# A paged-attention layer: new keys transposed by VectorE with the first queries, new values moved to matching partitions

## The chip, the cores and the metric

The kernel runs on one core of a Trainium2 chip. The metric is the device time of one launch in microseconds (us): the median of several runs. The engines of a core are TensorE (PE in the profile, with its weight loads as PEld), VectorE (DVE), ScalarE (ACT), GpSimd (POOL) and SyncE (SP, which here only issues DMAs). Sixteen DMA engines move data.

## The reference

Eight sequences of 128 tokens with 512 channels go through two residual layers, all in float32. The first adds a per-sequence adapter product (LoRA). The second is grouped-query attention over a paged cache: 32 query heads share 8 key and value heads, and every query sees up to 512 cached keys, those below the sequence's length, and its 128 new keys.

```python
w = weight[adapter_ids]                          # 512 x 512 for each sequence
x = x + einsum('bsi,boi->bso', x, w)
q, k, v = x @ Wq.T, x @ Wk.T, x @ Wv.T           # 32, 8, 8 heads of 128
q, k = rope(rmsnorm(q) * q_norm_w), rope(rmsnorm(k) * k_norm_w)
k_all = concatenate([k_cache[block_table], k])   # 512 cached + 128 new keys
v_all = concatenate([v_cache[block_table], v])
scores = q @ k_all.T * SCALE                     # masked beyond the length
o = softmax(scores) @ v_all                      # each kv head serves 4 query heads
x = x + o @ Wo.T
```

## The kernel before

The work is cut into 32 steps, 4 groups of heads times 8 sequences. A step (g, b) handles 8 query heads and 2 key/value heads (j = 0, 1) of one sequence. The main loop (L981) runs over the steps, and within a step over 8 slots, one for each query head h, where j = h // 4 and r = h % 4. Four heads with the same j form a unit.

In a slot TensorE first makes the head's scores (L1031): a matmul over the 512 cached keys and one over the 128 new keys. In the trace each of the float32 matmuls is two passes. VectorE adds the mask and finds the smallest score (L1041; the queries are negated). ScalarE takes the exponential (L1057), VectorE the reciprocal of the sum (L1098), and GpSimd scales (L1105). One slot later VectorE transposes the 128 x 640 result p in blocks of 32 x 32 (`turn_p`, L871). Such blocks don't make a full transpose: the blocks must still change partitions. So when the four heads of a unit are through, `send` (L889) writes them to DRAM, and in the next slot `receive` (L898) reads them back rearranged as pT, with keys on partitions. A value matmul needs pT (`values`, L825; named o<-pT).

The rest of TensorE's work fills the slots as a list of pieces, `main`: the projections of the next step (pj_kv, pj_q), the values of the step before (o), and its output product (out). A planner gives each piece a cost (`UNIT` = 0.86) and spreads the pieces evenly over the slots that are left. Small transposes are put at fixed slots by `at(step, slot, early, function, n)` with a cost of n x 0.11, which the planner counts.

There are two ways to transpose an operand. Cached keys and queries mostly go the way of p: VectorE turns 32 x 32 blocks, SyncE's DMA queue writes them to DRAM and reads them back (`send_k` L782, `receive_k` L796, `send_q` L804). The new keys instead go through TensorE: `turn_k` (L759) transposes one 128 x 128 head with the identity, and ScalarE copies it from PSUM into kT's last part (L764). It is called twice for each step, at slot 6 of the step before for j = 0 and at slot 2 for j = 1 (L266, L268). For the first, second and last step the queries too are turned by TensorE (`by_pe`, L637).

The block transposes leave the keys of a sequence in a particular order: after turning, key position i of block a comes from row 4i + a. In kT that order is a, c, i (block, chunk of 128 keys, position), and the mask, key_no and p have the same order. So the new keys have to be written in the matching order too. That is done in `rotate` (L639), where GpSimd adds the two halves of the rotary embedding with strided output (L671), the `turned_order` branch. The new values, vn, are copied by ScalarE as they are (L716).

Projections' follow-up work is put on a list, `pending`, and run at the next slot. DMA receives go on the list `to_read` with the slot they were asked in, and are issued a slot later, in order of a second number:

```python
due = [r for r in to_read if r[0] < 8 * i + h]
for _, _, f in sorted(due, key=lambda r: r[1]):
    f()
```

SyncE issues in program order and holds everything behind a DMA that still waits. Its order within a late step: in slot 0 the send of the second unit of the step before (xp) and kT for j = 1; in slot 1 that unit's pT and the send of the next step's cached keys (xk); in slot 3 the send of the next step's first queries (xq); in slot 4 the send of the first unit, the first queries' receive (qT) and the next kT for j = 0; in slot 5 the first unit's pT; in slot 6 the send of the second queries, and in slot 7 their receive. ScalarE issues the weight DMAs and GpSimd the gathers of cached keys and values.

Of the kernel before, what the change touches and what calls it, by code (L numbers as in the profile page):

```python
# [18 lines left out]
P = 128  # L19
# [33 lines left out]
def lora_then_paged_attention(  # L53
# [155 lines left out]
    for a in range(4):  # L209
# [9 lines left out]

    key_no = const.tile([P, 4, LC, Q4], FP, name="key_no")  # L220
    nc.gpsimd.iota(
        key_no,
        pattern=[[1, 4], [P, LC], [4, Q4]],
        base=0,
# [4 lines left out]
    nc.gpsimd.memset(mhalf, -0.5)  # L229
    masks = [const.tile([P, 4, NC, Q4], FP, name=f"mask_{n}") for n in range(2)]  # L230
    for m in masks:
        nc.gpsimd.memset(m[:, :, LC, :], 0.0)

# [154 lines left out]
    def rope_angles():  # L388
# [7 lines left out]
        def temp(tag):  # L396
            t = work.tile([P, 4, D], FP, tag=tag, name=f"rope_{tag}")
            return t.rearrange("p h (u d) -> p (h u) d", u=2)

# [200 lines left out]
    class Step:  # L600
        def __init__(self):
            self.kT, self.qT, self.q, self.pT, self.oT = {}, {}, {}, {}, {}
            self.scaled = set()

# [24 lines left out]
    def make_mask(i):  # L629

        b = steps[i][1]
        nc.vector.tensor_scalar(
            masks[i % 2][:, :, 0:LC, :], key_no, len_f[:, b : b + 1], FAR, ALU.is_ge, ALU.mult
        )
# [4 lines left out]
    def rotate(i, y, dst, ss, table, n, between=None):  # L639
# [11 lines left out]

        turned_order = i > 0 and (table == 1 or (i, n) in by_pe)
        cw = dst
        if turned_order and table:
            cw = sw[:, 2 : 2 + heads, :]
        elif turned_order:
            cw = work.tile([P, 4, D], FP, tag=f"tq{n}", name=f"cw_{i}_{n}")
        nc.vector.tensor_tensor(
# [22 lines left out]
    def norm_scales(i, n, width):  # L681
# [22 lines left out]
    def project(i, what):  # L704
# [3 lines left out]
        def after_kv(y):  # L708
            s.k = work.tile([P, GK, D], FP, tag="k", name=f"k_{i}")
            s.vn = news.tile([P, GW], FP, tag="vn", name=f"vn_{i}")  # L710
            s.ss = [
                small.tile([P, 6], FP, tag=f"ss{n}", name=f"ss_{i}_{n}") for n in range(2)
            ]

            def rest():
                nc.scalar.copy(s.vn, y[:, GW : 2 * GW])  # L716
                rotate(i, y, s.k, s.ss[0][:, 4:6], 1, 0)

            pending.append(rest)

        def after_q(n):
            def after(y):
                s.q[n] = work.tile([P, 4, D], FP, tag=f"q{n}", name=f"q_{i}_{n}")

                def rest():
                    rotate(
                        i,
                        y,
                        s.q[n],
                        s.ss[n][:, 0:4],  # L730
# [16 lines left out]
    def turn_kc(i, j, copy=None):  # L747

        s = st[i]
        s.kT[j] = work.tile([P, 4, NC, Q4], FP, tag=f"kT{j}", name=f"kT_{i}_{j}")  # L750
# [6 lines left out]
        (copy or nc.scalar.copy)(s.kT[j][:, :, 0:LC, :].rearrange("d a c i -> d c a i"), t)  # L757

    def turn_k(i, j, copy=None):  # L759
        s = st[i]  # L760
        t = ps_mm.tile([P, HID], FP, tag="mm", name=f"kt_{i}_{j}")
        t = t[:, 0:P].rearrange("d (i a) -> d i a", a=4)
        nc.tensor.transpose(t.rearrange("d i a -> d (i a)"), s.k[:, j, :], ident)  # L763
        (copy or nc.scalar.copy)(s.kT[j][:, :, LC, :].rearrange("d a i -> d i a"), t)  # L764

# [30 lines left out]
    def receive_k(i, j):  # L796
        s = st[i]
        s.kT[j] = work.tile([P, 4, NC, Q4], FP, tag=f"kT{j}", name=f"kT_{i}_{j}")
        nc.sync.dma_start(
            out=s.kT[j][:, :, 0:LC, :].rearrange("d b c k -> d b (c k)"),  # L800
            in_=s.xk[:, :, j, :].rearrange("b d x -> d b x"),
        )
# [171 lines left out]
    turn_q(0, 0, on_act)  # L974
    turn_k(0, 0, on_act)
    for _ in range(3):
# [4 lines left out]
    for i, (g, b) in enumerate(steps):  # L981
# [38 lines left out]
        for h in range(8):  # L1020
# [8 lines left out]
            sc = ps_sc.tile([P, 1024], FP, tag="sc", name=f"sc_{i}_{h}")  # L1029
            for lo, hi in ((0, L), (L, LA)):  # L1030
                nc.tensor.matmul(  # L1031
                    sc[:, lo:hi],
                    lhsT=s.qT[j][:, r, :, :].rearrange("d h q -> d (h q)"),
                    rhs=s.kT[j].rearrange("d a c i -> d (a c i)")[:, lo:hi],
                    start=True,
# [7 lines left out]
                in0=sc[:, 0:LA],  # L1043
                in1=masks[i % 2].rearrange("p a c i -> p (a c i)"),
                scale=1.0,
# [54 lines left out]
            if i == last and j == 1:  # L1100

                unit.p[r] = probs.tile([P, LA], FP, tag="p", name=f"pk_{h}")
                p = p.rearrange("q (a c i) -> q a c i", a=4, c=NC)
                q = unit.p[r].rearrange("q (c i a) -> q a c i", a=4, c=NC)
            nc.gpsimd.tensor_scalar(q, p, unit.rc[:, one], 1.0, ALU.mult, ALU.mult)  # L1105
# [77 lines left out]
```

## Time and profile before

| | |
|---|---|
| runs | 1197.11, 1199.97, 1198.83 us; median 1198.83 |
| profiled execution | 1197.03 us, span 1194.7 us |
| TensorE clock granted | 1.00 |
| VectorE busy | 733.6 us (61%) |
| ScalarE busy | 531.5 us (44%) |
| GpSimd busy | 674.9 us (56%) |
| DMA | 328.02 MB, mean 275 GB/s |
| queue 1 (SyncE's) | 239.23 MB, 59.6% of 16 engines' span |
| queue 10 (ScalarE's) | 48.12 MB, 12.4% |
| queue 0 (GpSimd's) | 39.86 MB, 10.1% |

A group in the profile reads: line, engine, operation, output<-inputs, shapes, count | busy us, mean ns of one | idle time of the engine before them, and what ended it. Busy time is the union of the durations, so overlapping instructions count once. A timeline row has start, duration, engine, line, operation, tensors and count. The row of a stretch has its bounds and length, then each engine's busy time and count (PE, PEld, DVE, ACT, POOL), the granted clock, the DMA engines' mean share and GB/s; this share sums the packets' durations, so packets that overlap on an engine can take it above 1.

### The profile page before, as it was taken

Reading aid. Unit: us, or ns where it says so; the run is one execution under the profiler, and the core shown is the slowest. Engines: PE = TensorE matmul, PEld = TensorE weight load, DVE = VectorE, ACT = ScalarE, POOL = GpSimd, SP = SyncE. Lnnn points to the kernel's source line nnn. Section 1 sums busy time; section 2 is a strip of 40 time slices with the busy share of each in tenths; the row PEclk is TensorE's granted clock in tenths of the full one; section 3 lists DMA queues with packets and bytes.
Section 4 is the critical chain, followed back from the end, with each engine's and each line's share of the span. In section 5 each row is a group of like instructions: output and inputs, shape, how many; then the busy total and the mean of one; then the engine's idle time right before and its main releaser. Section 6 shows DMA issues by size and latency. Waiting matters only on the chain.

```text
span 1194.7 us, 12971 instructions
## 1 busy us (share of the span) xinstructions
PE 1178.0 (99%) x3412; PEld 576.4 (48%) x3412; DVE 733.6 (61%) x1675; ACT 531.5 (44%) x1648; POOL 674.9 (56%) x781
## 2 busy tenths in 40 slices
PE   7899999999999999999999999999999999999998
PEld 4554455454444444444444444444444444444454
DVE  5566656665566666766566676666657655565651
ACT  4564444444444444444444444444444444444432
POOL 5566455545566556555655556565556556655540
PEclk9999999999999999999999999999999999999999
DMA  8388788877988988888998998888898987777761
GB/s 290 110 278 273 261 292 293 275 261 246 309 289 301 334 303 300 294 270 300 296 303 280 340 313 298 298 278 300 267 319 277 303 285 264 243 255 242 260 222 60
DMA packets 187148, 328.02 MB, mean 275 GB/s; under 512 B 13124, under 2 KB 106052, under 8 KB 178116
## 3 DMA queue, kind: packets, MB, share of 16 engines
q1 hardware_dynamic: 124272, 239.23, 59.6%
q10 hardware_dynamic: 49524, 48.12, 12.4%
q0 software_dynamic: 13280, 39.86, 10.1%
q8 instruction: 27, 0.44, 0.2%
q14 instruction: 45, 0.37, 0.1%
HBM read 195.04 MB, written 132.12 MB: 274 GB/s over the span
## 4 chain that ended last, share of the span: by engine, by line
PE 97%; DMA 1%; ACT 1%; DVE 0%; POOL 0%; issue 0%; ACTq 0%; DVEq 0%; POOLq 0%
PE o L559 23%; PE sc L1031 23%; PE pj_q L559 18%; PE out L559 18%; PE pj_kv L559 9%; PE y L559 2%; PE lw L474 1%; DMA w_q<-xw_q 1%; PE x L474 1%; PE kt L763 1%; PE wt_q L492 0%; PE wt_kv L492 0%; PE qt L772 0%; PE wt_o L492 0%; PE pt L881 0%
## 5 line engine op out<-in xcount | busy, mean ns | idle before, releaser
L1041 DVE CUSTOM_DVE_ANT_0 p<-sc,mask 128x640 f32<-128x640 f32 x256 | 210.9, 824 | 400.5 <-PE sc L1031 400.4
L1057 ACT ACTIVATE p<-p,mn 128x640 f32<-128x640 f32 x256 | 211.6, 827 | 324.6 <-DVE mn L1041 322.4
L1031 PE MATMUL sc<-kT,qT 128*128 128x512 f32 (+1 forms) x1024 | 318.4, 433 | 1.1 <-ACT kT L764 0.8
L1105 POOL TENSOR_SCALAR p<-p,rc 128x640 f32<-128x640 f32 x252 | 201.9, 801 | 183.0 <-DVE rc L1098 181.0
L1031 PEld LDWEIGHTS sc<-kT,qT 128*128 128x128 f32 x1024 | 189.9, 190 | 226.4 <-issue 206.0
L559 PE MATMUL pj_q<-w_q,x1T 128*128 128x512 f32 x512 | 236.9, 593 | 1.4 <-ACT w_q L493 0.7
L559 PE MATMUL o<-pT,vc 128*128 128x512 f32 x512 | 236.9, 593 | 0.0
L559 PE MATMUL out<-w_o,oT 128*128 128x512 f32 (+1 forms) x528 | 234.9, 580 | 0.9 <-ACT oT L838 0.7
L871 DVE STREAM_TRANSPOSE tp<-p 128x640 f32<-128x640 f32 x252 | 211.0, 837 | 4.9 <-POOL p L1105 4.7
L610 POOL DMA_INDIRECT kc<-in_L_cond_k_cache_dram,key_ix x128 | 130.8, 1022 | 32.7 <-issue 32.5
L610 POOL DMA_INDIRECT vc<-in_L_cond_v_cache_dram,val_ix x128 | 127.9, 999 | 31.0 <-issue 30.8
L692 ACT ACTIVATE q<-q,rs 128x128 f32<-128x128 f32 x256 | 81.9, 390 | 139.1 <-POOL q L679 134.5
L559 PEld LDWEIGHTS out<-w_o,oT 128*128 128x128 f32 x528 | 95.7, 190 | 93.5 <-issue 89.9
L559 PEld LDWEIGHTS pj_q<-w_q,x1T 128*128 128x128 f32 x512 | 92.4, 190 | 93.8 <-issue 91.4
L559 PEld LDWEIGHTS o<-pT,vc 128*128 128x128 f32 x512 | 91.9, 190 | 88.6 <-issue 81.3
L559 PE MATMUL pj_kv<-w_kv,x1T 128*128 128x512 f32 x256 | 116.6, 593 | 0.7 <-ACT x1T L476 0.7
L671 POOL TENSOR_TENSOR k<-sw 128x256 f32<-128x256 f32 x31 | 22.9, 739 | 157.1 <-PE kt L763 133.4
L679 POOL TENSOR_TENSOR q<-q,sw 128x512 f32<-128x512 f32 x59 | 74.7, 1266 | 45.0 <-DVE sw L662 44.9
L646 ACT ACTIVATE sq<-pj_q 128x128 f32<-128x128 f32 x256 | 70.8, 277 | 50.4 <-PE pj_q L559 41.5
L687 POOL TENSOR_TENSOR rs<-ss,mhalf 128x6 f32<-128x6 f32 x64 | 77.6, 1212 | 5.3
L559 PEld LDWEIGHTS pj_kv<-w_kv,x1T 128*128 128x128 f32 x256 | 45.9, 190 | 45.6 <-issue 44.7
L559 PE MATMUL o<-pT,vn 128*128 128x512 f32 x128 | 65.4, 593 | 0.0
(123 smaller groups left out, 873.6 us busy)
## 6 DMA issues: line engine op xcount, KB each, us to landing
xp<-tp SPq DMA_DIRECT2D x63, 1280.0 KB, 5.9
pT<-xp SPq DMA_DIRECT2D x63, 1280.0 KB, 7.0
xk<-tk SPq DMA_DIRECT2D x31, 512.0 KB, 7.5
kT<-xk SPq DMA_DIRECT2D x62, 256.0 KB, 6.6
xq<-tq SPq DMA_DIRECT2D x59, 256.0 KB, 4.6
qT<-xq SPq DMA_DIRECT2D x59, 256.0 KB, 5.2
st_q<-in_L_cond_Wq_dram ACTq DMA_DIRECT2D x24, 256.0 KB, 5.3
xw_q<-tw_q ACTq DMA_DIRECT2D x24, 256.0 KB, 4.4
```

What stands on the lines that cost most here:

```text
L474: nc.tensor.transpose(t[:, j, :], blk, ident)
L559: nc.tensor.matmul(y[0], lhsT=lhsT, rhs=rhs, start=(k == 0), stop=(k == len(pieces) - 1))
L610: nc.gpsimd.indirect_dma_start(out=dst[:, c, :], out_offset=None, in_=src, in_offset=bass.IndirectOffsetOnAxis(ap=rows[:, g, at : at + 1], ...
L646: nc.scalar.activation(sq, t[:, h, :], AF.Square, scale=float(D) ** -0.5, accum_out=ss[:, h : h + 1])
L679: add.tensor_tensor(dst, cw, sw[:, 0:heads, :], ALU.add)
L687: nc.gpsimd.tensor_tensor(rs[:, 0:width], ss[:, 0:width], mhalf[:, 0:width], ALU.pow)
L692: nc.scalar.activation(q, q, AF.Identity, scale=rs[:, h : h + 1])
L871: nc.vector.transpose(u.tp[:, :, r, :], u.p.pop(r).rearrange("q (a k) -> q a k", a=4))
L1031: nc.tensor.matmul(sc[:, lo:hi], lhsT=s.qT[j][:, r, :, :].rearrange("d h q -> d (h q)"), rhs=s.kT[j].rearrange("d a c i -> d (a c i)")[:, ...
L1041: nc.vector.tensor_tensor_reduce(out=p, in0=sc[:, 0:LA], in1=masks[i % 2].rearrange("p a c i -> p (a c i)"), scale=1.0, scalar=3.0e38, op0 ...
L1057: nc.scalar.activation(p, p, AF.Exp, bias=unit.mn[:, one], scale=-1.0, accum_out=unit.sm[:, one])
L1105: nc.gpsimd.tensor_scalar(q, p, unit.rc[:, one], 1.0, ALU.mult, ALU.mult)
```

## The change

The new keys no longer get a tile of their own. `rotate` writes them behind the four heads of the first queries, into a tile `q0` of six heads, and in natural order, so GpSimd's addition is a plain one (except in the steps of `by_pe`). `send_q(i, 0)` turns and sends all six heads; after the first queries' receive, a second DMA receives the two key heads into a new tile kn. TensorE's `turn_k` stays for the first, second and last step only, where it turns both heads and has one copy.

kT holds the cached keys alone. Scores now read kT and kn as two operands, the cached keys in the order c, a, i, and so do the mask, key_no and p; `turn_p` reads p in that order and writes what it wrote before. There is one mask tile instead of two. The new values must now match keys in natural order: ScalarE copies them to a tile vt, and four DMAs move 32 partitions each to every fourth partition of vn. They are issued by SyncE a slot after the copy. One transposition of the residual input (`turn_x1` for the last sequence) is put one slot earlier.

As built, TensorE has 6 key transposes instead of 64. In late steps the sixth head's scores come one value matmul earlier; otherwise its order is the same. SyncE issues 157 DMAs more (32 x 4 for values, 29 for keys).

```diff
         if i == 0:
             at(i, 2, False, lambda: turn_q(0, 1))
+            at(i, 6, False, lambda: turn_k(1), 2)
...
         if i == last:
+            at(i - 1, 6, False, lambda: turn_k(last), 2)
...
-        at(i, 2, True, lambda i=i: turn_k(i, 1), 1)
-        if i < last:
-            at(i, 6, False, lambda i=i: turn_k(i + 1, 0), 1)
...
-            at(i, 8 if i else 9, True, lambda b=b: turn_x1(b + 2))
+            at(i, (7 if b + 3 == B else 8) if i else 9, True, lambda b=b: turn_x1(b + 2))
...
-        turned_order = i > 0 and (table == 1 or (i, n) in by_pe)
+        turned_order = i > 0 and (i, n) in by_pe
...
                 for j in range(GK):
-                    nc.vector.tensor_scalar(
-                        s.k[:, j, :], s.k[:, j, :], rs[:, 4 + j : 5 + j], None, ALU.mult
-                    )
+                    k = s.q[0][:, 4 + j, :]
+                    nc.vector.tensor_scalar(k, k, rs[:, 4 + j : 5 + j], None, ALU.mult)
...
             def rest():
-                nc.scalar.copy(s.vn, y[:, GW : 2 * GW])
-                rotate(i, y, s.k, s.ss[0][:, 4:6], 1, 0)
+                vt = work.tile([P, GW], FP, tag="vt", name=f"vt_{i}")
+                nc.scalar.copy(vt, y[:, GW : 2 * GW])
+                for a in range(4):
+                    to_read.append(
+                        (
+                            now[0],
+                            2,
+                            lambda a=a: nc.sync.dma_start(
+                                out=s.vn.rearrange("(i a) x -> a i x", a=4)[a],
+                                in_=vt[Q4 * a : Q4 * a + Q4, :],
+                            ),
+                        )
+                    )
+                rotate(i, y, s.q[0][:, 4 : 4 + GK, :], s.ss[0][:, 4:6], 1, 0)
...
     def send_q(i, n):
         s = st[i]
-        tq = work.tile([P, 4, 4, Q4], FP, tag=f"tq{n}", name=f"tq_{i}_{n}")
+        heads = 4 if n else 4 + GK
+        tq = work.tile([P, 4, heads, Q4], FP, tag=f"tq{n}", name=f"tq_{i}_{n}")
         nc.vector.transpose(tq, s.q[n].rearrange("p h (a d) -> p a h d", a=4))
-        xq = xch.tile([4, P, 4, Q4], FP, tag=f"xq{n}", name=f"xq_{i}_{n}")
+        xq = xch.tile([4, P, heads, Q4], FP, tag=f"xq{n}", name=f"xq_{i}_{n}")
...
-                in_=xq.rearrange("b d h q -> d b (h q)"),
+                in_=xq[:, :, 0:4, :].rearrange("b d h q -> d b (h q)"),
             )
+            if n == 0:
+                nc.sync.dma_start(
+                    out=new_keys(i).rearrange("d b j q -> d b (j q)"),
+                    in_=xq[:, :, 4 : 4 + GK, :].rearrange("b d j q -> d b (j q)"),
+                )
...
-        nc.vector.transpose(u.tp[:, :, r, :], u.p.pop(r).rearrange("q (a k) -> q a k", a=4))
+        nc.vector.transpose(
+            u.tp[:, :, r, :].rearrange("q a (c i) -> q a c i", c=NC),
+            u.p.pop(r).rearrange("q (c a i) -> q a c i", c=NC, a=4),
+        )
...
-            for lo, hi in ((0, L), (L, LA)):
+            for lo, hi, keys in (
+                (0, L, s.kT[j].rearrange("d a c i -> d c a i")),
+                (L, LA, s.kn[:, :, j, :]),
+            ):
                 nc.tensor.matmul(
                     sc[:, lo:hi],
                     lhsT=s.qT[j][:, r, :, :].rearrange("d h q -> d (h q)"),
-                    rhs=s.kT[j].rearrange("d a c i -> d (a c i)")[:, lo:hi],
+                    rhs=keys,
```

New keys that TensorE still turns:

```python
def turn_k(i, copy=None):
    s = st[i]
    t = ps_mm.tile([P, HID], FP, tag="mm", name=f"kt_{i}")
    for j in range(GK):
        nc.tensor.transpose(t[:, j * P : (j + 1) * P], s.q[0][:, 4 + j, :], ident)
    (copy or nc.scalar.copy)(
        new_keys(i).rearrange("d b j q -> d j b q"),
        t[:, 0 : GK * P].rearrange("d (j b q) -> d j b q", j=GK, b=4),
    )
```

More of the change, by code (lines that the diff above doesn't have):

```diff
@@ L218, in lora_then_paged_attention @@
         nc.gpsimd.memset(quad[rows, :], float(a))
-    key_no = const.tile([P, 4, LC, Q4], FP, name="key_no")
+    key_no = const.tile([P, LC, 4, Q4], FP, name="key_no")
     nc.gpsimd.iota(
         key_no,
-        pattern=[[1, 4], [P, LC], [4, Q4]],
+        pattern=[[P, LC], [1, 4], [4, Q4]],
         base=0,
@@ L229, in lora_then_paged_attention @@
     nc.gpsimd.memset(mhalf, -0.5)
-    masks = [const.tile([P, 4, NC, Q4], FP, name=f"mask_{n}") for n in range(2)]
-    for m in masks:
-        nc.gpsimd.memset(m[:, :, LC, :], 0.0)
+    mask = const.tile([P, NC, 4, Q4], FP, name="mask")
+    nc.gpsimd.memset(mask[:, LC, :, :], 0.0)
     lora_ix = const.tile([P, B], I32, name="lora_ix")
@@ L396, in temp @@
         def temp(tag):
-            t = work.tile([P, 4, D], FP, tag=tag, name=f"rope_{tag}")
-            return t.rearrange("p h (u d) -> p (h u) d", u=2)
+            n = 4 + GK if tag in ("q0", "tq0") else 4
+            t = work.tile([P, n, D], FP, tag=tag, name=f"rope_{tag}")
+            return t[:, 0:4, :].rearrange("p h (u d) -> p (h u) d", u=2)
         ang, turns, sin, cos = temp("q0"), temp("q1"), temp("tq0"), temp("sw")
@@ L602, in __init__ @@
             self.kT, self.qT, self.q, self.pT, self.oT = {}, {}, {}, {}, {}
+            self.kn = None
             self.scaled = set()
@@ L632, in make_mask @@
         nc.vector.tensor_scalar(
-            masks[i % 2][:, :, 0:LC, :], key_no, len_f[:, b : b + 1], FAR, ALU.is_ge, ALU.mult
+            mask[:, 0:LC, :, :], key_no, len_f[:, b : b + 1], FAR, ALU.is_ge, ALU.mult
         )
@@ L656, in rotate @@
         elif turned_order:
-            cw = work.tile([P, 4, D], FP, tag=f"tq{n}", name=f"cw_{i}_{n}")
+            cw = work.tile([P, 4 if n else 4 + GK, D], FP, tag=f"tq{n}", name=f"cw_{i}_{n}")
+            cw = cw[:, 0:4, :]
         nc.vector.tensor_tensor(
@@ L708, in after_kv @@
         def after_kv(y):
-            s.k = work.tile([P, GK, D], FP, tag="k", name=f"k_{i}")
+            s.q[0] = work.tile([P, 4 + GK, D], FP, tag="q0", name=f"q_{i}_0")
             s.vn = news.tile([P, GW], FP, tag="vn", name=f"vn_{i}")
@@ L722, in after @@
             def after(y):
-                s.q[n] = work.tile([P, 4, D], FP, tag=f"q{n}", name=f"q_{i}_{n}")
+                if n:
+                    s.q[n] = work.tile([P, 4, D], FP, tag=f"q{n}", name=f"q_{i}_{n}")
                 def rest():
@@ L728, in rest @@
                         y,
-                        s.q[n],
+                        s.q[n][:, 0:4, :],
                         s.ss[n][:, 0:4],
@@ L749, in turn_kc @@
         s = st[i]
-        s.kT[j] = work.tile([P, 4, NC, Q4], FP, tag=f"kT{j}", name=f"kT_{i}_{j}")
+        s.kT[j] = work.tile([P, 4, LC, Q4], FP, tag=f"kT{j}", name=f"kT_{i}_{j}")
         t = ps_mm.tile([P, HID], FP, tag="mm", name=f"kct_{i}_{j}")
@@ L756, in turn_kc, with new_keys @@
             )
-        (copy or nc.scalar.copy)(s.kT[j][:, :, 0:LC, :].rearrange("d a c i -> d c a i"), t)
-    def turn_k(i, j, copy=None):
+        (copy or nc.scalar.copy)(s.kT[j].rearrange("d a c i -> d c a i"), t)
+    def new_keys(i):
         s = st[i]
[L761 to L764, printed above, removed]
+        if s.kn is None:
+            s.kn = turned.tile([P, 4, GK, Q4], FP, tag="kn", name=f"kn_{i}")
+        return s.kn
+    def turn_k(i, copy=None):
+        s = st[i]
+        t = ps_mm.tile([P, HID], FP, tag="mm", name=f"kt_{i}")
+        for j in range(GK):
+            nc.tensor.transpose(t[:, j * P : (j + 1) * P], s.q[0][:, 4 + j, :], ident)
+        (copy or nc.scalar.copy)(
+            new_keys(i).rearrange("d b j q -> d j b q"),
+            t[:, 0 : GK * P].rearrange("d (j b q) -> d j b q", j=GK, b=4),
+        )
     def turn_q(i, n, copy=None):
@@ L797, in receive_k @@
         s = st[i]
-        s.kT[j] = work.tile([P, 4, NC, Q4], FP, tag=f"kT{j}", name=f"kT_{i}_{j}")
+        s.kT[j] = work.tile([P, 4, LC, Q4], FP, tag=f"kT{j}", name=f"kT_{i}_{j}")
         nc.sync.dma_start(
-            out=s.kT[j][:, :, 0:LC, :].rearrange("d b c k -> d b (c k)"),
+            out=s.kT[j].rearrange("d b c k -> d b (c k)"),
             in_=s.xk[:, :, j, :].rearrange("b d x -> d b x"),
@@ L870, in turn_p @@
             u.tp = turned.tile([P, 4, REP, QK], FP, tag="tp", name=f"tp_{u.i}_{u.j}")
-        nc.vector.transpose(u.tp[:, :, r, :], u.p.pop(r).rearrange("q (a k) -> q a k", a=4))
+        nc.vector.transpose(
+            u.tp[:, :, r, :].rearrange("q a (c i) -> q a c i", c=NC),
+            u.p.pop(r).rearrange("q (c a i) -> q a c i", c=NC, a=4),
+        )
     def turn_p_pe(u, r):
@@ L974, in lora_then_paged_attention @@
     turn_q(0, 0, on_act)
-    turn_k(0, 0, on_act)
+    turn_k(0, on_act)
     for _ in range(3):
@@ L1043, in lora_then_paged_attention @@
                 in0=sc[:, 0:LA],
-                in1=masks[i % 2].rearrange("p a c i -> p (a c i)"),
+                in1=mask.rearrange("p c a i -> p (c a i)"),
                 scale=1.0,
@@ L1102, in lora_then_paged_attention @@
                 unit.p[r] = probs.tile([P, LA], FP, tag="p", name=f"pk_{h}")
-                p = p.rearrange("q (a c i) -> q a c i", a=4, c=NC)
-                q = unit.p[r].rearrange("q (c i a) -> q a c i", a=4, c=NC)
+                p = p.rearrange("q (c a i) -> q c a i", a=4, c=NC)
+                q = unit.p[r].rearrange("q (c i a) -> q c a i", a=4, c=NC)
             nc.gpsimd.tensor_scalar(q, p, unit.rc[:, one], 1.0, ALU.mult, ALU.mult)
```

## The prediction

> **What bounds the kernel now.** I read the page first (engines, chain), then the busy time by stretch, then the timeline of TensorE, and last the DMA queue of SyncE.
>
> ```profile
> PE 1178.0 (99%) x3412; PEld 576.4 (48%) x3412; DVE 733.6 (61%) x1675; ACT 531.5 (44%) x1648; POOL 674.9 (56%) x781
> ...
> PE 97%; DMA 1%; ACT 1%; DVE 0%; POOL 0%; issue 0%; ACTq 0%; DVEq 0%; POOLq 0%
> ```
>
> TensorE is busy for 99% of the span, and 97% of the chain that ended last is its own. By stretch:
>
> ```profile
> 300.00:500.00 200.00, 199.53 (x543) 94.53 (x542) 130.61 (x297) 87.92 (x285) 117.32 (x132) 1.00 0.92 306
> 500.00:700.00 200.00, 199.76 (x543) 94.57 (x542) 129.01 (x295) 87.51 (x278) 121.43 (x137) 1.00 0.91 301
> 900.00:1100.00 200.00, 200.00 (x544) 94.79 (x543) 121.33 (x288) 87.17 (x284) 118.02 (x133) 1.00 0.81 266
> ```
>
> The second number is TensorE's busy time: it lacks at most half a microsecond in 200. The last two columns are the DMA engines' share and GB/s: 0.92 where weights are also being turned, 0.81 later. So work taken from TensorE pays in full, as long as the DMA engines, the next fullest resource, don't make it wait.
>
> What is one transpose of new keys worth? Two views answer differently:
>
> ```profile
> L763 PE MATMUL kt<-ident,k 128*128 128x128 f32 x64 | 17.4, 273 | 0.0
> ```
>
> ```profile
> 602.63 0.81 PE L1031 MATMUL sc<-kT,qT 128*128 128x512 f32 x3
> 603.28 0.27 PE L763 MATMUL kt<-ident,k 128*128 128x128 f32 x1
> 603.39 0.59 PE L559 MATMUL o<-pT,vc 128*128 128x512 f32 x1
> ```
>
> The group says 273 ns each, 17.4 us for 64. The timeline shows the next matmul starting 0.11 us after the transpose: durations overlap. Six pj_q passes of 512 columns last 2.74 us together, so they start (2.74 - 0.59)/5 = 0.429 us apart. A late step has 76 passes of 512 columns and 18 of 128: 76 x 0.429 + 18 x 0.107 = 34.5 us, and the steps' first scores start 34.62 us apart. So the transpose costs 0.107 us.
>
> [...] the new key rows are 256 B. Before has only one 256 B packet (18 ns, beside a median of 27 ns for 512 B)[...]. [...]
>
> **The change part by part**, against the profiled execution: 1197.03 us, span 1194.7.
>
> *Transposes removed.* As built, 6 key transposes stay (steps 0, 1 and the last), 58 go: 58 x 0.107 = 6.2 us, all on the path. Their 64 ScalarE copies of 387 ns become 3; ScalarE is 44% busy, so this earns nothing directly. The first scores waited 0.8 us for such a copy at 40.8 us; now two transposes and one wider copy stand there: +0.1 us.
>
> *Strided keys as moving operand.* Scores now read kT in runs of 32 elements. pj_q already reads w_q in such runs at 593 ns, and scores read contiguous keys at 593 ns: cost nothing. The order of p changes likewise: turn_p now reads 32-element runs. tk<-kc (runs of 32) and tq<-q both take 670 ns for 512 elements, 1.31 ns each, and 640 x 1.31 = 837 is what tp<-p takes: nothing.
>
> *VectorE.* tq0 grows from 512 to 768 elements: 256 x 1.31 = 0.335 us, 29 times. In that slot VectorE sits idle 1.90 us before the next scores (timeline, 612.6 us): hidden. Uncovered it would be 9.7 us. GpSimd's key addition takes 719 ns in plain order (one case) against 739 turned: nothing. One mask instead of two: its write follows VectorE's own last read in order, so no new wait.
>
> *DMA work.* Per step: the new keys' send adds 1 KB to each of 128 packets (2 KB: 84 ns; by the sizes' medians about 38 ns more); 512 packets of 256 B at 18 to 27 ns; 128 packets of 1 KB for values at 46 ns. Over 16 engines: 0.30 + 0.58 (to 0.86) + 0.37 = 1.25 us, to 1.5, in 34.6. A share of 0.92 becomes about 0.96, and queue 1 carries (29 + 29 + 32) x 0.131 = 11.8 MB more.
>
> *Queue positions.* SyncE issues five more DMAs a step, at 0.36 us each 1.8 us. The four for values come a slot after ScalarE's copy; behind them waits the next step's query send, which is about 5 us away: hidden. The new keys' receive stands behind the first queries' receive and waits for the same landing, so its wait is not new; behind it stand kT and the first pT, 0.45 us later. I matched these landings with first use: kT has at least 3.6 us, the first unit's pT 6 to 12 us in full steps. The keys themselves are due half a step later.
>
> *The tight place* is the second unit's pT:
>
> ```profile
> 423.07 0.33 SPq L889 DMA_DIRECT2D xp<-tp  x1
> 423.49 0.39 SPq L799 DMA_DIRECT2D kT<-xk  x1
> 431.52 0.36 SPq L898 DMA_DIRECT2D pT<-xp  x1
> ```
>
> This send took 8.4 us, the receive 7.1: landed at 438.6. Its first use:
>
> ```profile
> 438.82 1.02 PE L559 MATMUL pj_q<-w_q,x1T 128*128 128x512 f32 x2
> 439.68 2.74 PE L559 MATMUL o<-pT,vc 128*128 128x512 f32 x6
> ```
>
> 1.07 us were left. Over the 23 second units with a recorded landing the slack is 0.92, 1.07, 1.36, 1.44, 1.54, 1.65, 1.84, 1.93, 2.40, 2.85, then over 3. If all land d later, the stall is the sum of d - slack: d = 1 gives 0.1 us, 1.25 gives 0.5, 2 gives 4.3; times 31/23 for all steps. Nothing is added just before this pair; the additions stand 15 us earlier[...]. So d lies between 0 and 1.25 us, the whole DMA work added; I take about 1.1, 0.4 us in all.
>
> *Schedule.* One value matmul moves behind the sixth scores in late steps; TensorE's sum is the same. The x1 transposes of the last batch move a slot earlier:
>
> ```profile
> 281.34 2.84 PE L559 MATMUL pj_kv<-w_kv,x1T 128*128 128x512 f32 x6 [0.67 <-ACT x1T L476]
> ```
>
> That wait goes, with the start after it: -0.8 us. TensorE also waited some 0.5 us each at 321 and 598 us for w_q, in steps that receive twelve weights. More traffic can lengthen that: +0.4, between 0 and 2.
>
> Sum: -6.2 + 0.1 - 0.8 + 0.4 + 0.4 = -6.1, so 1190.9 for a profiled execution. The median of runs, 1198.83, is 1.8 above that execution; the four times average 1198.2. Taken from there: 1192.1, say 1192.
>
> **Rivals.**
> - *The group's duration is the price*: 58 x 0.273 = 15.8 us, less the small terms: 1182.5. The timeline speaks against it. 0.03.
> - *The gain is eaten*: pT lands about 2 us later and w_q costs 2 us. 5.7 + 2 against 7.0 gained: 1197 to 1199. For it: DMA shares of 1.07 in single 10 us stretches, where a little more work may delay much. Against: 1.25 us of work is no 2 us of delay, unless contention multiplies it. 0.11.
> - *Slower: the second unit's pT becomes TensorE's bound.* Place: the first value matmul of each step's second half. At d = 3 us the stall is 13.0 x 31/23 = 17.5 us, less 7.0: 1208.7. It decides from d = 2.1 on, and passes 0.2% from about 2.35. For it: ten slacks under 3 us and a DMA share of 0.92 before. Against: landings varied by 5 us already (5.7 to 10.9) and TensorE hardly waited. 0.12.
> - *The forecast*: 0.74.
>
> **How the numbers follow.** A measurement here tells about 0.2% (2.4 us) from no change; the limit is 1196.4. The forecast's own range is 1189 to 1195.5, its ends the unknown terms at 0 and 3 us with the runs' spread. It and the first rival are faster (0.77), and a little of the second (0.02); the rest of the second is no change (0.09); the third, with its milder cases, is slower (0.12). Below 1189 lie some 0.05; reaching up to 1199 takes in the second rival and leaves out about 0.12 above.
>
> **What would show it.** Right: kt x6, TensorE busy near 1171, late steps 34.41 us apart, stretches still without idle TensorE, queue 1 near 251 MB, VectorE busy near 743 us. Wrong: waits of o on DMA pT or on the send before it; longer waits of pj_q on w_q; scores waiting for kn or kT (SyncE's queue); scores' passes further apart than 0.429 us (strided keys cost); tp<-p above 837 ns.

## The result, and the profile after

| | median, us | runs | ratio to before, 95% interval |
|---|---|---|---|
| before | 1198.32 | 1196.63 to 1199.97 | |
| after | 1211.05 | 1203.25 to 1215.07 | 1.0103 [1.0067, 1.0140] |

Both medians are of six runs. The change makes the kernel about 1% slower; I had forecast 1192. The profiled execution of after is the shortest of its six runs: 1203.25 us, span 1201.4.

The page of the changed kernel, busy time and chain:

```profile
PE 1174.7 (98%) x3354; PEld 571.5 (48%) x3354; DVE 742.3 (62%) x1675; ACT 515.8 (43%) x1587; POOL 677.3 (56%) x780
...
PE 88%; DMA 6%; issue 2%; DVE 1%; ACT 1%; SPq 1%; POOL 0%; ACTq 0%; DVEq 0%; POOLq 0%
```

TensorE executes 58 matmuls fewer and its busy time is down by 3.3 us, yet its share of the chain falls from 97% to 88%: DMA and SyncE's queue now have a part in what ends last. The same stretches as before show where:

```profile
300.00:500.00 200.00, 196.22 (x521) 92.20 (x520) 128.74 (x286) 82.21 (x262) 118.14 (x132) 0.99 0.94 309
500.00:700.00 200.00, 198.44 (x533) 93.62 (x532) 131.85 (x298) 85.85 (x275) 117.31 (x132) 1.00 0.94 311
900.00:1100.00 200.00, 200.00 (x537) 94.31 (x536) 124.77 (x292) 84.99 (x272) 120.14 (x134) 1.00 0.86 284
```

From 900 us on TensorE still has no idle time. From 300 to 500 us it lacks 3.8 us, and the granted clock is 0.99. The first scores of late steps tell whether a step got shorter:

```profile
946.46 1.02 PE L1069 MATMUL sc<-kT,qT 128*128 128x512 f32 x2
...
980.86 1.02 PE L1069 MATMUL sc<-kT,qT 128*128 128x512 f32 x2
...
1015.26 1.02 PE L1069 MATMUL sc<-kT,qT 128*128 128x512 f32 x2
```

They are 34.40 us apart, against 34.62 before: undisturbed steps gained what was forecast. So the loss is in single places. The waits of TensorE (total, times, longest):

```profile
PE pj_q L558 <- DMA w_q<-xw_q: 5.8, 3, 2.5
PE sc L1069 <- DMA qT<-xq: 1.9, 2, 1.0
PE out L558 <- DMA w_o<-xw_o: 1.7, 2, 1.3
PE sc L1069 <- issue: 1.4, 1, 1.4
```

In before, only one wait of TensorE was put down to a DMA, and no scores waited for one:

```profile
PE pj_q L559 <- DMA w_q<-xw_q: 0.2, 1, 0.2
```

In this execution of after no value matmul waits for pT, the place where I had put the danger.

Adding up what TensorE's starts lose beyond 0.838 ns per column (0.429 us for 512; gaps over 60 ns, from the first scores on) gives 6.3 us in before and 18.4 in after: pj_q 1.2 and 8.3, sc 1.6 and 5.4, out 1.4 and 3.6, all others 2.1 and 1.1. That is 12.1 more; less the 6.2 gained, 5.9 of the 6.7 us by which the span grew.

Of pj_q's 8.3, a part comes after the wait. The timeline and the stretches around the first of these waits:

```profile
321.84 0.38 PE L1069 MATMUL sc<-kn,qT 128*128 128x128 f32 x2
324.75 5.40 PE L558 MATMUL pj_q<-w_q,x1T 128*128 128x512 f32 x8 [2.53 <-DMA w_q<-xw_q]
```

```profile
324.00:325.00 1.00, 0.25 (x1) 0.25 (x2) 1.00 (x2) 0.11 (x2) 0.63 (x1) 1.00 0.93 230
325.00:326.00 1.00, 1.00 (x2) 0.26 (x2) 0.81 (x3) 0.00 (x0) 0.10 (x1) 0.70 0.79 204
326.00:327.00 1.00, 1.00 (x3) 0.47 (x2) 0.00 (x0) 0.00 (x0) 0.71 (x1) 0.50 0.64 170
...
329.00:330.00 1.00, 1.00 (x4) 0.39 (x3) 0.00 (x0) 0.00 (x0) 0.00 (x0) 1.00 0.99 420
```

Eight passes take 5.40 us here and 3.60 where nothing disturbs them. The clock's column falls to 0.50 after the idle time, by the clock's record from 325.40 us on, for 3.41 us: the wait of 2.5 us costs another 1.7. The mean clock of after's six runs goes from 0.999 (1203.3 us) to 0.994 (1215.1 us), where the profiled execution of before has 1.00 throughout. If all that the mean lacks were such windows (1.7 us each), 0.994 would be 4 of them, some 7 us; that is an estimate. But the two middle runs (1208.99 and 1213.11 us) have 0.997 and 0.998, which is 2 to 4 us, and the profiled one already has 1.7. So by the same estimate the windows themselves explain only 1 to 2 of the 7.8 us by which after's median lies above its profiled execution; the rest of it is not shown.

### The profile page after: what moved, and what is told of

It reads as the page before. It is cut to its first block, busy times and chain, and to the rows that moved or that the text cites. A ratio compares the mean times of both kernels' runs of the same rounds, so it can differ in the third digit from the quotient of the medians.

```text
span 1201.4 us, 12850 instructions
## 1 busy us (share of the span) xinstructions
PE 1174.7 (98%) x3354; PEld 571.5 (48%) x3354; DVE 742.3 (62%) x1675; ACT 515.8 (43%) x1587; POOL 677.3 (56%) x780
## 3 DMA queue, kind: packets, MB, share of 16 engines
q1 hardware_dynamic: 145728, 251.04, 62.2%
## 4 chain that ended last, share of the span: by engine, by line
PE 88%; DMA 6%; issue 2%; DVE 1%; ACT 1%; SPq 1%; POOL 0%; ACTq 0%; DVEq 0%; POOLq 0%
PE o L558 21%; PE sc L1069 21%; PE pj_q L558 17%; PE out L558 16%; PE pj_kv L558 8%; DMA w_q<-xw_q 3%; PE y L558 2%; DMA w_o<-xw_o 2%; DMA qT<-xq 1%; PE lw L473 1%; SPq L725 1%; PE x L473 1%; ACT sq L647 0%; DMA xq<-tq 0%; PE wt_kv L491 0%
## 5 line engine op out<-in xcount | busy, mean ns | idle before, releaser
L1069 PE MATMUL sc<-kT,qT 128*128 128x512 f32 x512 | 262.0, 593 | 4.0 <-DMA qT<-xq 1.9
L1069 PEld LDWEIGHTS sc<-kn,qT 128*128 128x128 f32 x512 | 97.2, 190 | 122.5 <-issue 121.2
L681 POOL TENSOR_TENSOR q<-q,sw 128x512 f32<-128x512 f32 (+1 forms) x89 | 96.7, 1086 | 102.7 <-DVE sw L664 102.5
L1069 PEld LDWEIGHTS sc<-kT,qT 128*128 128x128 f32 x512 | 94.5, 190 | 113.3 <-issue 108.9
L1069 PE MATMUL sc<-kn,qT 128*128 128x128 f32 x512 | 98.3, 274 | 0.0
```

The source lines that it names most:

```text
L681: add.tensor_tensor(dst, cw, sw[:, 0:heads, :], ALU.add)
L1069: nc.tensor.matmul(sc[:, lo:hi], lhsT=s.qT[j][:, r, :, :].rearrange("d h q -> d (h q)"), rhs=keys, start=True, stop=True,)
```

## The experiments

Each kernel was timed in rounds beside before. "Theory 1" in the first eight is that the new DMAs cost by their number and their place in SyncE's queue, above all the four value moves. Its rivals are the bytes and packets, and operands read in short runs; the second receive (of the keys) is tested as well. To make room, some of the kernels keep the norm weights in a tile that is shared with other data.

**First the parts of the change.** No value moves; TensorE reads the new keys in the old order instead, every fourth element.

```diff
-                vt = work.tile([P, GW], FP, tag="vt", name=f"vt_{i}")
-                nc.scalar.copy(vt, y[:, GW : 2 * GW])
...
+                nc.scalar.copy(s.vn, y[:, GW : 2 * GW])
...
-                (L, LA, s.kn[:, :, j, :]),
+                (L, LA, s.kn[:, :, j, :].rearrange("d b (u a) -> d a b u", a=4)),
```

> The changed kernel without the four value DMAs: values are copied straight to vn, and the scores read the new keys with a stride of four elements so that keys and values match. The changed kernel stands some 19 us above the 1192 us that its removed transposes allow. Theory 1 (the number of added DMAs: SyncE's issue time and DMAs waiting for earlier ones make receives late): 128 of 157 added DMAs are gone, the new keys' late receive in early steps stays (about 4 us): 1194 to 1198 us. Rival 2 (the DMA engines' time, bytes and packets): 0.37 of 1.25 us of added work is gone: 1203 to 1207 us. Rival 3 (operands read in short runs slow TensorE): 1205 us or more, with score passes further apart than 0.429 and 0.107 us; the stride of four would show the same way.

Measured: 1246.79 us, 1.0401 [1.0381, 1.0421]. A miss, by something else than what was asked:

```profile
502.49 0.60 PE L1057 MATMUL sc<-kn,qT 128*128 128x128 f32 x2
502.92 2.33 PE L558 MATMUL out<-w_o,oT 128*128 128x512 f32 x5
```

Two passes over the new keys take 0.43 us from start to start, where 0.22 is usual (317.32 to 317.54 in after). 512 passes x 0.107 = 55 us; without them 1192. Single floats 16 B apart cost double here, while runs of 32 floats cost nothing (kT's passes last 593 ns in before and in after). Why the stride costs was not shown.

Queries and new keys received by one DMA instead of two:

```diff
-            s.kn = turned.tile([P, 4, GK, Q4], FP, tag="kn", name=f"kn_{i}")
+            both = turned.tile([P, 4, 4 + GK, Q4], FP, tag="qk", name=f"qk_{i}")
+            s.qT[0], s.kn = both[:, :, 0:4, :], both[:, :, 4 : 4 + GK, :]
...
+                nc.sync.dma_start(
+                    out=s.qk.rearrange("d b h q -> d b (h q)"),
+                    in_=xq.rearrange("b d h q -> d b (h q)"),
+                )
```

> The changed kernel with first queries and new keys received by one DMA in runs of 768 B into one tile with two buffers, instead of 512 B and 256 B by two; the value DMAs stay. (For room, the norm weights use a tile that is free at the start and key_no is int16.) Theory 1 (number of DMAs): 29 of 157 are gone, but the waits of the first scores in steps 3, 4 and 6 (1.5 + 1.2 + 1.0 us) should go: 1203 to 1208 us. Rival 2 (bytes and packets): about 0.25 of 1.25 us of work is gone: 1206 to 1209 us, waits of steps 3, 4, 6 shorter but there. Rival 3 (operands): no change, 1211 us.

Measured: 1209.57, 1.0081 [1.0051, 1.0112], which can't be told from after: it lies above theory 1's range and just above that of the bytes. The keys' own receive is not the main cost.

Both edits together:

> Both edits: no value DMAs, one receive for queries and new keys, so no DMA more than the kernel before, and 256 KB more traffic a step. Theory 1 (number of DMAs): 1190 to 1194 us, below the kernel before, TensorE's clock at 1.00 throughout. Rival 2 (bytes and packets): about half of the added DMA work remains: 1198 to 1203 us. Rival 3 (operands read in short runs): 1205 us or more.

Measured: 1247.25, 1.0402 [1.0379, 1.0424]; less 55 again 1192, and TensorE waits for no DMA. This doesn't test the forecast, since slower scores also give every transfer more time.

**The value moves alone, put into before.** Four moves of vn to a spare tile, in the place where the change has them:

```diff
+                vd = work.tile([P, GW], FP, tag="vd", name=f"vd_{i}")
+                for a in range(4):
+                    to_read.append(
+                        (
+                            now[0],
+                            2,
+                            lambda a=a: nc.sync.dma_start(
+                                out=vd.rearrange("(i a) x -> a i x", a=4)[a],
+                                in_=s.vn[Q4 * a : Q4 * a + Q4, :],
+                            ),
+                        )
+                    )
```

> The kernel before, plus the four value DMAs alone: vn is also moved to a spare tile that nothing reads, so TensorE's work and all operands are those of before. Theory 1 (number of DMAs): 1205 to 1212 us, with waits of pj_q on w_q and a clock below 1.00. Rival 2 (bytes): 0.37 us of DMA work a step: 1200 to 1204 us. Rival 3: 1198 us, no change.

Measured: 1202.33, 1.0038 [1.0023, 1.0053]. That is the range of the bytes, not theory 1's, and about a third of what the moves cost in after; why they cost more there was not tested. Scores now wait for qT:

```profile
PE sc L1043 <- DMA qT<-xq: 3.6, 3, 1.8
```

The same bytes in one DMA (`out=vd, in_=s.vn`), and four DMAs of 8 of the 256 columns (`[:, 0:8]`):

> The kernel before, plus one DMA a step that moves vn's 128 KB to a spare tile, at the place where four DMAs of 32 KB cost 4.2 us (1202.3). Theory 1 (number: SyncE's issue time of 0.5 to 1.4 us each and waits for DMAs eight places earlier): 1198 to 1200 us. Rival 2 (bytes): the bytes are the same, so 1202 us.

> The kernel before, plus four DMAs a step that move only 8 of 256 columns each (1 KB instead of 32 KB). Theory 1 (number): 1201 to 1203 us, as with the full ones. Rival 2 (bytes): 1198 to 1199 us.

Measured: one move 1198.37, 0.9998 [0.9983, 1.0012]; four small ones 1201.53, 1.0032 [1.0019, 1.0045]. 4 KB in four DMAs cost about what 128 KB in four cost, and 128 KB in one cost nothing. It is the number, not the bytes. (The one DMA also leaves each row in its partition, where the four move rows to every fourth one. No run has one DMA with the strided target or four without it.)

**The keys' part alone.** After without value moves; so that keys and values match, VectorE turns p in two instructions, the last 128 columns with a stride of four (and for the p that TensorE turns, GpSimd scales these columns apart).

```diff
+            u.tp[:, :, r, 0 : LC * Q4].rearrange("q a (c i) -> q a c i", c=LC),
+            p[:, 0:L].rearrange("q (c a i) -> q a c i", c=LC, a=4),
+        )
+        nc.vector.transpose(
+            u.tp[:, :, r, LC * Q4 : QK], p[:, L:LA].rearrange("q (i a) -> q a i", a=4)
```

> The changed kernel without the value DMAs, made to match in another way: TensorE reads the new keys in runs of 32 as in the changed kernel, and VectorE turns p in two instructions, the 512 cached columns as in the changed kernel and the 128 new columns with a stride of four elements (about 0.1 to 0.2 us more per head on VectorE, which is idle 0.5 us or more in every slot). In the earlier run with values unmoved, the stride on TensorE cost 512 passes x 0.107 us = 55 us, so 1247 - 55 = 1192 is what it would have been without. Theory 1 (number of added DMAs, mostly the values'): 1191 to 1196 us, with a little waiting for qT or kn in steps 3, 4 and 6. Rival 2 (bytes): the new keys' 0.88 of 1.25 us of DMA work stays: 1202 to 1208 us.

The same with one receive as above:

> The same, with first queries and new keys received by one DMA into one double-buffered tile: no DMA more than the kernel before. Theory 1: 1190 to 1193 us, at or below the run with two receives, clock 1.00. Rival 2 (bytes): 1199 to 1205 us.

Measured: 1197.41, 0.9988 [0.9978, 0.9998], and 1196.21, 0.9982 [0.9969, 0.9994]. Faster than before, but by 1 to 2 us where 6 to 7 were due, outside the ranges of both theories, and with the same three waits on w_q (5.9 us in the first of the two). So there are two losses: one from the value moves, and one that stays without them.

**The second loss.** Before, with 62 of its 64 transposes simply left out; nothing is added:

```diff
-        at(i, 2, True, lambda i=i: turn_k(i, 1), 1)
-        if i < last:
-            at(i, 6, False, lambda i=i: turn_k(i + 1, 0), 1)
+        if i == 0:
+            at(i, 2, True, lambda i=i: turn_k(i, 1), 1)
```

> The kernel before with 62 of its 64 transposes of new keys on TensorE left out, and nothing put in their place: later steps score the new keys of the first step, which leaves out part of the computation. 62 x 0.107 = 6.6 us less on TensorE, no DMA more. Theory 1 (what is taken from TensorE pays in full, the keys' part alone loses its gain to the traffic and waits it adds): ratio 0.9945, 1191.5 to 1192.5 where before has 1198.5. Rival (TensorE reaches the twelve-weight steps earlier and then waits for w_q, so part of the gain is given back whatever else is done): 1193.5 to 1196, with pj_q waiting on w_q 1 us or more three times.

Measured: 1194.50, 0.9969 [0.9957, 0.9981]. Theory 1 fell for this part: 6.6 us of pure work removed gained 3.7 (0.0031 of before). The timeline of this kernel:

```profile
870.64 1.24 PE L1032 MATMUL sc<-kT,qT 128*128 128x512 f32 x4
874.08 5.37 PE L558 MATMUL pj_q<-w_q,x1T 128*128 128x512 f32 x8 [2.19 <-issue]
879.28 1.02 PE L1032 MATMUL sc<-kT,qT 128*128 128x512 f32 x2
```

TensorE comes to the first query projection with the next group's weights before the last of them has landed; it waits 2.2 us, and then its eight passes take 5.37 us, 1.77 more than the undisturbed 3.60; the mean clock of this execution is 0.998. (The view names no cause. By the events that tell of landings, a w_q transfer landed at 873.99, and pj_q starts at 874.08.) The three such places lose 6.0 us of starts, against 1.2 in before. In these steps (6 and 7 of each group) the DMA engines' share is above 1 for 15 us on end (1.12, 1.07, 1.11 from 305 to 320 us; 1.04, 1.09, 1.06 in before). That a shorter step asks for the same weights from engines that have no more to give fits this, but is argued.

**The first loss: number, queue or place?** After with one move of 128 KB (values stay in their rows' order, which doesn't match the keys'); after with the four moves issued by GpSimd; after with the four moves four slots later.

```diff
+                to_read.append(
+                    (now[0], 2, lambda: nc.sync.dma_start(out=s.vn, in_=vt))
+                )
```

```diff
-                            lambda a=a: nc.sync.dma_start(
+                            lambda a=a: nc.gpsimd.dma_start(
```

```diff
-                            now[0],
+                            now[0] + (4 if i >= 2 else 0),
...
-            to_read[:] = [r for r in to_read if r[0] == 8 * i + h]
+            to_read[:] = [r for r in to_read if r[0] >= 8 * i + h]
```

> The changed kernel with one DMA of 128 KB a step for the new values in place of four of 32 KB; the values then keep their rows' order, which doesn't match the keys' (a changed result, the same amount of work). Theory 1 (the number of DMAs that SyncE issues costs, not their bytes): near the kernel that changes the keys alone, 1196 to 1200. Rival (bytes and their round trip cost on top of the keys' traffic): 1205 to 1212, near the changed kernel.

> The changed kernel with the four moves of new values issued by GpSimd's queue instead of SyncE's; same bytes, same number. Theory 1 (they cost by standing in SyncE's queue, ahead of kT, pT and the queries' receive, and by the semaphores that this queue shares with ScalarE's): 1196 to 1201; scores no longer wait for qT in steps 3, 4 and 6. Rival (their traffic, or a landing that comes late on any queue): 1205 to 1212. If GpSimd's own work becomes late through them: above 1212.

> The changed kernel with the four moves of new values issued four slots later from step 2 on, still by SyncE. Theory 1a (their place ahead of kT and pT of the same slots costs): 1197 to 1202. Theory 1b (their number in SyncE's queue costs wherever they stand, through the semaphores that come round earlier): 1206 to 1212, as the changed kernel.

Measured: one move 1198.12, 0.9997 [0.9980, 1.0015]. By GpSimd 1205.94, 1.0057 [1.0036, 1.0079]: about half of the loss stays, and theory 1's range (1196 to 1201) was missed for its rival's. TensorE there waits for what GpSimd itself gathers (vc 1.4 us, lraw 1.4) and still 1.6 for qT; how much each of these costs was not taken apart. Later 1198.31, 0.9998 [0.9987, 1.0010]: the same four moves in the same queue, in another slot, cost nothing that shows beyond the keys' part. So number and place act together, and theory 1b, that they cost wherever they stand, fell.

The profile of the kernel with the later moves puts 3.3 us of pj_q's waiting down to vn<-vt; by the events in its trace that tell of landings, the last of the w_q transfers that pj_q needs landed at 321.49, and pj_q starts at 321.58. So this is the wait for w_q again.

What the place does is seen ahead of step 3. SyncE's queue in before:

```profile
141.49 0.37 SPq L799 DMA_DIRECT2D kT<-xk  x1
148.98 0.37 SPq L816 DMA_DIRECT2D qT<-xq  x1
```

In after:

```profile
140.02 0.33 SPq L924 DMA_DIRECT2D xp<-tp  x1
140.45 3.77 SPq L725 DMA_DIRECT2D vn<-vt  x4
144.32 0.54 SPq L824 DMA_DIRECT2D kT<-xk  x1
145.63 0.33 SPq L836 DMA_DIRECT2D xq<-tq  x1
146.05 0.39 SPq L933 DMA_DIRECT2D pT<-xp  x1
148.80 0.37 SPq L843 DMA_DIRECT2D qT<-xq  x1
```

and with the moves later:

```profile
140.51 0.38 SPq L824 DMA_DIRECT2D kT<-xk  x1
145.67 0.32 SPq L836 DMA_DIRECT2D xq<-tq  x1
146.16 0.37 SPq L933 DMA_DIRECT2D pT<-xp  x1
148.27 0.37 SPq L843 DMA_DIRECT2D qT<-xq  x1
```

Issuing four moves takes 3.77 us, and the receive of kT, right behind them, starts 3.8 us later. The DMA engines have less to do meanwhile; the last two columns of these stretches are their share and GB/s, first in after, then with the moves later:

```profile
144.00:147.00 3.00, 3.00 (x8) 1.33 (x7) 2.62 (x4) 1.12 (x3) 0.28 (x1) 1.00 0.68 219
147.00:150.00 3.00, 3.00 (x9) 1.36 (x8) 1.75 (x4) 1.12 (x4) 2.54 (x3) 1.00 0.89 255
```

```profile
144.00:147.00 3.00, 3.00 (x8) 1.32 (x8) 2.67 (x4) 1.15 (x3) 0.24 (x1) 1.00 0.94 292
147.00:150.00 3.00, 3.00 (x9) 1.38 (x9) 1.75 (x4) 1.31 (x5) 2.54 (x3) 1.00 1.01 278
```

That is (292 - 219 + 278 - 255) x 3 = 288 KB not moved: about one kT (256 KB). (In the 3 us before, after had moved 132 KB more, the value moves themselves.) qT is issued at the same time as in before, but the scores that need it start after an idle TensorE:

```profile
157.76 1.10 PE L1069 MATMUL sc<-kT,qT 128*128 128x512 f32 x2 [1.36 <-issue]
```

By the same kind of events qT lands at 154.9 in before, at about 156.0 with the moves later and at 157.7 in after. kT lands at 147.6, 146.4 and 147.8. So what the moves' place costs is measured, but that kT's bytes push qT back is argued: kT lands hardly later in after than in before. In late steps nothing is close behind the moves:

```profile
957.52 2.52 SPq L725 DMA_DIRECT2D vn<-vt  x4
966.65 0.34 SPq L836 DMA_DIRECT2D xq<-tq  x1
```

and there they cost nothing.

Are there waits behind this? The traces record updates of semaphores, counters that here tell of the landing of a DMA. The 709 DMAs that SyncE and ScalarE issue in after use eight of them, and the two engines' orders of issue fit together so that the eight come in turn, all 709 times (in before all 552). In after 328 of these issues, 72 of them of value moves, wait on the semaphore that they use themselves, so for the DMA that had it eight places earlier; in before 192 do. Some of the waits hold the queue. After's waits of SyncE contain

```profile
SPq L725 <- DMA pT<-xp: 7.8, 2, 4.0
```

though the moves need nothing of pT: one stands still from 402.98 to 407.00, until the pT that had its semaphore before it (issued at 399.82) has landed, at 406.99. ScalarE's receive of w_o stands for 3.2 us close by (406.63 to 409.78), and the output product waits for w_o at 422 us. In before only one receive of w_o was held so, for 0.7 us. With the moves later their waits for pT are longer (14.5 us, three times) and yet the kernel is faster (1198.31 beside 1211.05): a held queue cost here only by what stood behind it. The durations of the issues (469 to 2089 ns for one value move) are not these waits: in after the last update of the semaphore comes before the recorded start of every such issue. Why four moves take 3.77 us ahead of step 3 stays open, and no run takes the semaphores' waits away.

**Are these the two losses?** The receives of the next group's query weights were reordered: the last three of the first half one slot earlier, the second half one slot later.

```diff
-                read_at(before + 8 * (B - 2) + (2, 4, 6)[k] + n, (kind, g, n))
+                late = (n, max(n - 1, 0), n + 1)[k]
+                read_at(before + 8 * (B - 2) + (2, 4, 6)[k] + late, (kind, g, n))
```

In before without transposes; in after with the moves later (with two tiles in turn for vt); in before; in the keys' part with one receive:

> The kernel before without 62 of its 64 transposes of new keys (as in the run that left them out: later steps score stale new keys), and with the receives of the next group's weights reordered: the last three of the first query half one slot earlier, the four of the second half one slot later. If half of the 6.6 us was given back because TensorE now comes to the first query projection before these weights: no wait of pj_q on w_q above 0.5 us, clock 1.000, 1190.5 to 1192.5, ratio 0.994. If it was given back elsewhere: 1194 to 1195 again, 0.997.

> The changed kernel with its value moves four slots later, two tiles in turn for the values that wait to be moved, and the same reordering of the weights' receives. If the changed kernel's two losses are its place in SyncE's queue and the weights' lateness, and nothing else of weight: what was forecast for the change, 1191 to 1194, ratio 0.995. If the contention of 157 more DMAs or the value moves themselves hold a share: 1195 to 1199.

> The kernel before with that reordering alone. Its waits on w_q were about 0.5 us twice, so at most 1 us is to be had: 1197 to 1198.5, ratio 0.999 to 1.000. If the weights' lateness costs more in most executions than in the profiled one (half-speed windows after it): up to 2 us, 1196.

> The kernel with the keys' part alone, one receive for queries and keys, and that reordering. Without it the ratio was 0.9982. Waits on w_q of 1.5 to 1.8 us three times would go: 1191 to 1193, ratio 0.995. If the DMA engines are simply full in those steps and the wait only moves to other tiles (qT, w_kv, second half of w_q): 1195 to 1197.

Measured: 1193.78, 0.9954 [0.9937, 0.9971]; 1193.10, 0.9971 [0.9942, 0.9999]; 1198.06, 0.9997 [0.9982, 1.0012]; 1194.49, 0.9967 [0.9955, 0.9979]. Before itself gains nothing by it. The others come out 0.0015 (without transposes), 0.0027 (moves later) and 0.0015 (keys' part) better than without it, none of them clear of the intervals; the first and the last lie between what I had expected of the two theories. In the profiled execution of the first the delayed second half was waited for 4.6 us once, so the delay is a risk of its own. Hence the last two: after with the reordering alone; and after with the moves later, two tiles for vt and only the first half's receives earlier (`late = (n, max(n - 1, 0), n)[k]`).

> The changed kernel with the reordering of the weights' receives alone; the value moves stay where they were in SyncE's queue. If the two losses simply add (14 us for the value moves' place, about 3 to 5 for the weights): 1206 to 1208, ratio 1.006 to 1.008. If the late weights and their half-speed windows are mainly a consequence of the value moves' place: at most 2 us less than the changed kernel, 1209 to 1211. If the value moves' place only hurts by way of the weights: 1195 to 1200.

> The changed kernel with later value moves, two value tiles, and only the first query half's last three receives one slot earlier; the second half's receives stay in their slots, since in the run that delayed them without the transposes the second half was waited for 4.6 us once. If that delay is a risk of its own: no wait on w_q above 1 us, 1191 to 1193.5, and fewer runs above 1195. If the first half needs the second half out of its way: waits of 1 to 2 us on w_q again, 1194 to 1197.

| after, with | median, us | ratio to before |
|---|---|---|
| nothing else | 1211.05 | 1.0103 [1.0067, 1.0140] |
| weights reordered | 1205.19 | 1.0061 [1.0042, 1.0080] |
| moves later | 1198.31 | 0.9998 [0.9987, 1.0010] |
| moves later, two tiles, first half of the weights earlier | 1193.32 | 0.9956 [0.9942, 0.9970] |

By the ratios, the weights are worth 0.0042 alone and the moves 0.0105 alone, 0.0147 in sum. Moves later with the same reordering gave 0.0132 (0.9971), with the first half alone 0.0147. So within the intervals the two losses add; the exact match of the last is luck, since the interval of after alone is 0.007 wide. Both combined kernels also have the second tile for vt, which no run separates: with one tile ScalarE's copy into vt once waited 7.05 us for the moves. The last kernel beats before by 5 us. Its profile:

```profile
PE 1172.4 (99%) x3354; PEld 570.9 (48%) x3354; DVE 744.2 (63%) x1675; ACT 515.3 (43%) x1587; POOL 673.0 (57%) x780
...
319.22 3.70 PE L559 MATMUL pj_q<-w_q,x1T 128*128 128x512 f32 x8 [0.19 <-DMA w_q<-xw_q]
```

The query projection waits 0.2 us for the weights and starts 5.5 us earlier than in after. The span is 1189.1 us, and TensorE's lost starts from the first scores on are 6.4 us, as in before (6.3).

## Why the prediction was wrong, point by point

- *Transposes, -6.2.* Right as a price: 6 are left, and steps are 34.40 us apart (34.41 foretold). TensorE's busy time is 1174.7 us where I expected 1171; part of that is passes at half clock (1172.4 in the last kernel). Wrong was "pays in full": a gain that brings TensorE to a transfer before it has landed is given back there (of the 6.6 us of transposes left out 3.7 were gained).
- *Strided keys, order of p, VectorE.* Right: scores' passes 593 and 274 ns, tp<-p 837 ns, VectorE 742.3 us (743). The turned query tile of 768 elements took 937 ns, 267 more than that of 512, not 335.
- *DMA work.* Right in size: 251.04 MB on queue 1 as foretold, share 0.94 (0.96 foretold). A mean share said nothing on single steps.
- *Queue positions, "hidden".* The failed step, 12.7 us (1211.05 - 1198.31): I put the value moves' place in SyncE's queue at nothing. I priced an issue at 0.36 us and the next transfer behind the moves at 5 us away. The moves took 0.47 to 2.09 us each (the keys' receive 0.50 to 2.20), and the 5 us were read in a late step; in the first group kT stands right behind them, ahead of steps 3 to 6. I also asked whether each transfer would land in time for itself. kT did; what came late was qT, two receives further.
- *"The keys themselves are due half a step later."* The keys' second receive was no main cost (one receive: 1.0081 beside 1.0103).
- *w_q, +0.4 (0 to 2).* Mis-sized: up to 5.0 us (1198.31 - 1193.32, the second tile for vt included), with 1.7 us of half clock behind a wait. Where the weights' order alone was changed, it brought 0.0042 in after and 0.0015 in the keys' part. I took traffic for its cause. Leaving the transposes out without any traffic brings it too.
- *Second unit's pT, +0.4.* No such wait came in the profiled execution. (The sum was off too: by the slacks listed, a delay of 1.1 us gives 0.3.) The slower rival named this place and its 1208.7 is near the result, but its mechanism didn't happen.
- *x1's wait, -0.8.* Right, it is gone. First scores: they start 0.3 us earlier, not 0.1 later.
- *From profile to median, +1.1.* In after it is 7.8. Half-clock windows explain 1 to 2 of it. The half pace at the start that the last section shows, 4.9 us without a mark in the clock, may be a part too; the one trace of after starts at full pace.

The loss of 12.7 us is one of medians. The two profiled executions differ by 4.6 only (1203.25 and 1198.65), of which starts of sc are 4.2 (5.4 and 1.2) and of out 2.2 (3.6 and 1.4), with pj_q 2.4 the other way. The rest lies in executions of after that left no trace but a lower mean clock (0.994 to 0.998).

What stays open: which waits grow in those executions; how an issue that is held makes qT land late; why the weights' landing doesn't move earlier with the slots that ask for it (the full DMA engines are argued, from their share); what share the semaphores' waits have; and what the moves cost on GpSimd's queue.

## What to carry to other kernels

Time taken from the busiest engine is worth its price only as far as the next transfer that this engine meets: list the waits that were just met (0.2 to 0.5 us here), and move those transfers earlier together with the change. A few tiny DMAs in an in-order queue are priced, by these runs, not by their bytes (four of 1 KB 1.0032, four of 32 KB 1.0038, one of 128 KB 0.9998) but by what stands right behind them, in the earliest and fullest steps as well as in the typical one; ask also what happens to the transfer after the next. Where half clock follows a late transfer, as it did once in after, a stall of 2.5 us costs over 4.

## What the runs showed of the hardware

- *Half clock after a short idle.* In after an idle time of 2.53 us (up to 324.75 us) was followed by 3.41 us at a granted clock of 0.50; there passes of 512 columns start 0.853 us apart, where 0.429 is usual at 1.00. After 2.21 us of idle time in the same execution (up to 883.14 us) the clock stayed at 1.00 and the passes 0.429 us apart. Without transposes eight passes took 5.37 us instead of 3.60 after 2.19 us; with the weights reordered there, six took 4.54 instead of 2.74 after 4.64. What decides between the cases is not shown.
- *Half pace without a mark.* Some executions (with the values on GpSimd, and of the keys' part alone) run matmuls between 12 and 23 us at about half pace while the granted clock reads 1.00. With the values on GpSimd the profiled one did:

```profile
13.36 3.67 PE L473 MATMUL lw<-ident,raw_lora 128*128 128x128 f32 x16
```

  The same 16 take 1.97 us in after, eight passes of 512 columns right behind them 3.67 instead of 6.11, and the first scores start at 45.4 instead of 40.5 us. Profiled spans of single executions can so differ by 4.9 us; the verdicts above rest on medians.
- *Every fourth float.* On VectorE the strided turn of 128 elements took 369 ns and the other 512 took 704, where all 640 in runs took 837.
